# The first batch's work as one flat list of steps, in a quantized gated feed-forward kernel

## The chip, the cores and the metric

The kernel runs on one core of one Trainium2 chip. The metric is the device time in microseconds of one execution; a kernel's time is the median of its runs. The engines are named PE (matrix engine), PEld (its weight loads), ACT (scalar engine), DVE (vector engine), POOL (GpSimd) and SP (sync engine, which here only issues transfers). Each engine takes its instructions strictly in the order in which the program issues them to that engine, and waits at an instruction until what it needs is ready.

## The reference

Four batches of 1024 tokens, 512 wide, go through one gated feed-forward layer of 2048 hidden features whose hidden activations and down weights are quantized:

```python
scale = cond @ norm_w.T + 1.0
ms = jnp.mean(x * x, axis=-1, keepdims=True)
h = x * (scale[:, None, :] * jax.lax.rsqrt(ms + EPS))
u = h @ up_w.T
val, gate = jnp.split(u, 2, axis=-1)
h = val * jax.nn.gelu(gate, approximate=False)
hq = act_quant(h)       # per token: round(h * 127 / max|h|), clipped, scaled back
wq = weight_quant(down_w)   # round(w / mean|w|) to -1, 0, 1, times mean|w|
y = hq @ wq.T
return y + x
```

`x` is (4, 1024, 512), `cond` (4, 128), `norm_w` (512, 128), `up_w` (4096, 512), `down_w` (512, 2048), all float32.

## The kernel before

The hidden features are cut into 16 tiles `j` of 128 (`NJ`), the tokens of a batch into two halves `h` of 512. A slot is the work of one tile for one batch; `g = 16 * b + j` counts slots. Every float32 operand of the up projection is split into a high and a low float16 part, so that one product is three float16 products. PE sets the pace: from slot 14 on (`FAST = NJ - 2`) a slot does seven products (a Strassen scheme over the two token halves and gate and value; `product`, line 652) instead of the eight of the plain form (`plain`, line 667), and each later batch works its down projection in between.

The first batch, `b = 0`, is where everything else is prepared, beside PE:

- **Weights of tile j.** `w_load` (SP) brings them, `w_range` takes the largest or the sum of absolute values per row (from tile 3 on by ACT, line 304) and derives a power-of-two factor (`w_factor`, DVE, lines 161, 313, 319), `w_gain` makes the gains (DVE, lines 334, 337), `w_scale` scales the rows (ACT, line 349), `w_rows` splits them into high and low (ACT line 374, DVE line 375) and has them transposed by a transfer (SP, line 376) into one of three buffers `s_tile(j)`.
- **Sums for the fast form.** `s_sums` forms four sums of the weight blocks (POOL; DVE for tiles 14 and 15; lines 402 to 405) in a single scratch `sf`, `s_high` and `s_low` split them (ACT line 422, POOL line 426), `s_spill` writes all seven blocks to `s_dram`. Later batches read them back with `s_load`, in four pieces per slot.
- **Token sums of batch 0** for its two fast slots: `t0_whole` (line 677), `t0_sum` (680), `t0_high` (683) and `t0_low` (686), placed by the table `T0_STEPS` in slots 4 to 14.
- **Tokens of batch 1**, in four groups `a` of 128 pairs: class `Tokens` (load, norm, scale, sums, high, low, turn; lines 567 to 627). `turn` is one transposing transfer.
- **Conditioning rows of batches 1 to 3**: `cond_load_rest` broadcasts three rows of `cond` to all partitions (ACT's queue, line 182), `cond_scale_rest` multiplies and reduces them against `norm_w` on DVE (lines 203, 204) in slot 1; `cond_largest`, `cond_over`, `cond_range`, `cond_spread`, `cond_undo` and `cond_rows` turn them into scales.
- **Down weights**: `d_load`, `d_sum` (ACT, line 492) and `d_total`, `d_mean` find the mean; `d_fetch`, `d_round`, `d_sign` quantize.
- **Running maxima of the hidden values**: `pair_max` (DVE, lines 806 and 808).

One plain half-slot is `plain_half(j, h)`: twelve matmuls for the gate into a PSUM bank, the gelu of it on ACT (line 711), twelve matmuls for the value into another bank, and one DVE instruction that multiplies the two (line 715). The gate's bank is of tag B (one buffer) for half 0 and of tag A (two buffers) for half 1; the value's is of tag E (two buffers). So the gate of half 0 of a slot waits for the gelu of half 0 of the slot before, and a value waits for the DVE product of the half two before.

The order of the work around PE is written by hand: slots 1 and 2 line by line, slots 3 to 13 by the function `first_batch(j, sc)`, slots 14 and 15 by `first_fast(j)`. Where a helper has several instructions, they go out together: `w_range` issues ACT's sums and at once the DVE steps that need them, and `s_all` issues `s_high`, `s_low` and `s_spill` of a tile in a row. Ahead of slot 1 stands the head: loads, conditioning of batch 0, norms and transposes of the first 512 tokens, and filler matmuls (`keep_warm`, line 1079). Slots 16 to 63 and the end of the kernel have a planner of their own, which the change does not touch.

## Time and profile before

| | |
|---|---|
| median of 3 runs | 736.34 us (735.82 to 738.83) |
| the profiled execution | 737.17 us, span 735.4 us |
| granted PE clock, mean | 0.997 |
| PE busy | 718.5 us (98%), 3666 matmuls |
| DVE, ACT, POOL busy | 590.7, 419.4, 204.8 us |
| HBM read, written | 53.69 MB, 23.09 MB |

The span goes from the first to the last instruction of the profiled execution; the execution's own time is 1.8 us longer. A busy share is an average over stages with different limits, so the stretch that the change touches (about 21 us to 190 us of the span) is to be read by itself. In the rows of the profile, `L667` is a line of the kernel, `H<-pv,sg,g` are the tiles written and read, `x27` is a count, and `<-DVE H L715` names what ended a wait. SPq and ACTq are the issuing of transfers on SP's and ACT's queues.

### The profile page before, as it was taken

The numbers are of one execution on the slowest core, as the hardware profiler recorded it, in microseconds if no ns is written. First come the engines' busy times: TensorE is split into PE (matmuls) and PEld (weight loads), VectorE is DVE, ScalarE is ACT, GpSimd is POOL, SyncE is SP. The second block draws the span as 40 slices with busy tenths as digits, with TensorE's granted clock in tenths as the row PEclk, the third lists the DMA queues.
The fourth block names the chain that finished last, engine by engine and source line by source line (L and its number), as shares of the span: only waits on it lengthen the run. The fifth ranks groups of instructions, "written<-read, shape, count | busy, mean of one in ns | idle before, by whom it ended". The sixth has DMA issues, their size and how long they took to land.

```text
span 735.4 us, 10237 instructions
## 1 busy us (share of the span) xinstructions
PE 718.5 (98%) x3666; PEld 359.4 (49%) x3666; DVE 590.7 (80%) x828; ACT 419.4 (57%) x687; POOL 204.8 (28%) x201
## 2 busy tenths in 40 slices
PE   8999989989899999999999999999999999999998
PEld 3544434434344445665444444666444444444854
DVE  7855988979689889797679898687679888765896
ACT  6779657665666776544434667453333666333463
POOL 1477898783010030460010030452020000000120
PEclk9999999999999999999999999999999999999999
DMA  9689796989997546856955456666955464443243
GB/s 319 205 239 266 249 214 191 261 225 214 238 239 144 129 100 173 200 139 181 209 117 104 110 129 163 156 164 156 218 111 101 101 103 104 103 104 111 97 161 131
DMA packets 228542, 122.82 MB, mean 167 GB/s; under 512 B 189814, under 2 KB 199943, under 8 KB 228492
## 3 DMA queue, kind: packets, MB, share of 16 engines
q1 hardware_dynamic: 228202, 121.85, 66.5%
q8 instruction: 28, 0.46, 0.3%
q10 hardware_dynamic: 290, 0.33, 0.1%
q14 instruction: 22, 0.18, 0.1%
HBM read 53.69 MB, written 23.09 MB: 104 GB/s over the span
## 4 chain that ended last, share of the span: by engine, by line
PE 80%; POOL 6%; DVE 6%; DMA 2%; SPq 2%; issue 2%; ACT 1%; POOLq 0%; DVEq 0%; ACTq 0%
PE A L652 33%; PE E L652 17%; PE po L962 9%; PE B L652 8%; PE po_end L914 4%; PE pg L667 4%; PE pv L667 4%; DVE gm L806 1%; DMA H<-in_x_dram 1%; POOL R L426 1%; SPq L627 1%; POOL H L405 1%; POOL H L404 1%; DMA s_dram<-s_rows 1%; POOL xt L597 1%
## 5 line engine op out<-in xcount | busy, mean ns | idle before, releaser
L652 PEld LDWEIGHTS <-SXY 128*128 128x128 f16 x2058 | 201.4, 98 | 239.9 <-issue 3.3
L652 PE MATMUL A<-R,SXY 128*128 128x512 f16 x1158 | 268.2, 380 | 2.0 <-DMA SXY<-s_dram 2.0
L652 PE MATMUL E<-R,SXY 128*128 128x512 f16 x582 | 142.2, 380 | 0.3 <-DMA SXY<-s_dram 0.2
L770 DVE SCALAR_TENSOR_TENSOR H<-A,sg,t 128x512 f32<-128x512 f32 x50 | 37.5, 750 | 70.8 <-PE A L652 70.6
L822 POOL PARTITION_ALL_REDUCE am<-R x8 | 14.3, 1793 | 237.1 <-DVE R L808 237.1
L886 DVE TENSOR_TENSOR H<-H,am 128x1024 f32<-128x1024 f32 x64 | 76.1, 1215 | 0.0
L783 ACT ACTIVATE t<-t,sg 128x512 f32<-128x512 f32 x50 | 36.1, 721 | 67.6 <-DVE t L780 67.5
L652 PE MATMUL B<-R,SXY 128*128 128x512 f16 x294 | 71.5, 379 | 0.0
L667 PEld LDWEIGHTS <-SXY 128*128 128x128 f16 x438 | 42.7, 98 | 58.0 <-issue 7.0
L806 DVE TENSOR_REDUCE gm<-H 128x512 f32<-128x1024 f32 x56 | 69.0, 1233 | 1.1
L767 ACT ACTIVATE t<-B,sg 128x512 f32<-128x512 f32 x50 | 34.4, 687 | 37.8 <-PE B L652 37.8
L667 PE MATMUL pg<-R,SXY 128*128 128x512 f16 x228 | 52.4, 379 | 2.3 <-ACT g L711 2.3
L962 PE MATMUL po<-wd,R 128*128 128x256 fp8e4 x416 | 52.4, 273 | 0.0
L667 PE MATMUL pv<-R,SXY 128*128 128x512 f16 x210 | 48.9, 379 | 3.0 <-DVE H L715 3.0
L545 POOL TENSOR_SCALAR ssq<-ssq 128x2 f32<-128x2 f32 x12 | 3.4, 285 | 169.6 <-ACT xt L575 120.8
L750 ACT COPY t<-A 128x512 f32<-128x512 f32 x50 | 29.0, 580 | 34.4 <-PE A L652 34.1
L762 ACT COPY v<-E 128x512 f32<-128x512 f32 x50 | 29.3, 585 | 33.5 <-PE E L652 29.8
L962 PEld LDWEIGHTS <-R 128*128 128x128 bf16 (+1 forms) x448 | 43.8, 98 | 8.9
L757 ACT COPY B<-A 128x512 f32<-128x512 f32 x50 | 28.6, 572 | 29.1 <-PE A L652 28.6
L789 DVE SCALAR_TENSOR_TENSOR H<-v,sg,t 128x512 f32<-128x512 f32 x50 | 39.5, 791 | 6.3 <-ACT t L783 6.3
L808 DVE TENSOR_TENSOR R<-R,gm 128x512 f32<-128x512 f32 x56 | 42.6, 760 | 1.3
L894 ACT ACTIVATE H<-H 128x1024 f32<-128x1024 f32 x38 | 39.9, 1050 | 5.2 <-DVE H L886 5.2
(234 smaller groups left out, 1022.8 us busy)
## 6 DMA issues: line engine op xcount, KB each, us to landing
SXY<-s_dram SPq DMA_DIRECT2D x48, 256.0 KB, 3.1
H<-in_L_cond_up_w_dram SPq DMA_DIRECT2D x13, 512.0 KB, 4.6
s_dram<-SXY SPq DMA_DIRECT2D x17, 384.0 KB, 3.2
SXY<-s_dram SPq DMA_DIRECT2D x48, 128.0 KB, 3.2
xr<-in_x_dram SPq DMA_DIRECT2D x19, 256.0 KB, 3.0
out_dram<-xr SPq DMA_DIRECT2D x19, 256.0 KB, 2.4
H<-in_x_dram SPq DMA_DIRECT2D x8, 512.0 KB, 7.2
R<-in_L_cond_down_w_dram SPq DMA_DIRECT2D x8, 512.0 KB, 8.0
```

The lines of the kernel that those rows point to most:

```text
L652: PE.matmul(o, s[:, w, k, :], operand(g // NJ, c, l, k), start=start and n == 0, stop=stop and n == len(TERMS) - 1, skip_group_check=True,)
L667: PE.matmul(ps, a[k // 2][:, w, k % 2, :], XP[:, l, k, h * TOK : (h + 1) * TOK], start=n == 0, stop=n == len(terms) - 1,)
L767: ACT.activation(cur["t1"], pb, AF.Gelu, scale=gain(g, 1))
L770: DVE.scalar_tensor_tensor(h_half(g - 1, 0), prev["A"], gain(g - 1, 0), prev["t1"], ALU.mult, ALU.mult)
L783: ACT.activation(prev["t2"], prev["t2"], AF.Gelu, scale=gain(g - 1, 1))
L789: DVE.scalar_tensor_tensor(h_half(g - 1, 1), prev["v"], gain(g - 1, 0), prev["t2"], ALU.mult, ALU.mult)
L806: DVE.tensor_reduce(gm[0], v, AX.X, ALU.max, apply_absolute_value=True)
L808: return [largest, lambda: DVE.tensor_tensor(m, m, gm[0], ALU.max)]
L886: DVE.tensor_tensor(v, v, r.to_broadcast([P, 2, TOK]), ALU.mult)
L894: ACT.activation(v, v, AF.Copy, bias=MAGIC)
L914: PE.matmul(po.rearrange("p (y c o) -> p y c o", c=2, o=P), q[:, a, h, j], wd8[:, :, j // n, j % n, :, y0:y1].rearrange("p c o y -> p y c o"),
L962: PE.matmul(po, w[:, j], m, start=start and j == 0, stop=stop and j == n - 1, skip_group_check=True,)
```

## The change

The hand-written order from behind the first slot to the end of slot 15 is replaced by one flat list, `FIRST_BATCH`, that `take` walks through: each word is a step, with its arguments (`gate.4.1` is the gate of tile 4, half 1; `s_sum.5.1.1` is sum 1 of tile 5 on DVE, without the last 1 on POOL; `o_whole`, `o_sum`, `o_high`, `o_low` are the token sums of batch 0; `max` is `pair_max`; `c_...` are the conditioning steps; `slot.14.6` is step 6 of slot 14). The helpers are cut into single instructions for it: `s_sums` becomes four `s_sum`, `s_high`, `s_low` and `s_spill` take a part, `w_range` is apart from `w_factor`, `plain_half` becomes `half_gate`, `half_gelu`, `half_value` and `half_out`, `slot` uses a class `Slot` with the same products in the same order. PE's order of products is the one of before.

By the list, 37 of the 64 `s_sum`, 19 of the 32 `s_low` and 11 of the 16 `t_sum` are on DVE (before: 8 sums, and no `s_low` of the list's tiles). The token sums of batch 0 stand in slots 1 to 4 and use other scratch. `w_gain` from tile 3 on is on ACT. The first tokens of batch 1 and several weight tiles are loaded earlier; a number of spills stand later.

In the head, all four rows of `cond` are loaded at once, `norm_w` and `cond` are transposed on PE (`cond_turn`), and `cond_scale_rest` is four matmuls and one ACT instruction there; the broadcast load and the two DVE instructions of slot 1 are gone. From tile 3 on, `w_factor` writes the masked exponent beside a constant and takes the larger of the two by a reduction.

```diff
     ux = cpool.tile([P, B], F32, name="ux")
     nw = R[:, 1, 0:512].rearrange("p (k c) -> p k c", k=NK)
-    cb = R[:, 1, 512:1024].rearrange("p (b c) -> p b c", b=B)
+    nwT = R[:, 1, 512:1024]
     dots = R[:, 1, 1024 : 1024 + C]
...
-
+
+    def cond_turn():
+
+        pt = bank("E", 2, name="pc_t")
+        PE.transpose(pt[:, :B], cn, ident[:B, :B])
+        ACT.copy(cT, pt[:, :B])
+        pt = bank("E", 2, name="nw_t")
+        for k in range(NK):
+            PE.transpose(pt[:, k * P : (k + 1) * P], nw[:, k], ident)
+        ACT.copy(nwT, pt)
+
+    def cond_scale_rest():
+
+        n = B - 1
+        ps = bank("E", 2, name="ps")[:, : NK * n]
+        for k in range(NK):
+            PE.matmul(
+                ps[:, k * n : (k + 1) * n], nwT[:, k * P : (k + 1) * P], cT[:, 1:B],
+                start=True, stop=True,
+            )
+        v = ps.rearrange("p (k b) -> p k b", b=n)
+        ACT.activation(scT[:, :, 1:], v, AF.Copy, bias=1.0)
...
-    def cond_scale_rest():
-
-        n = B - 1
-        v = H[:, 9:11].rearrange("p s h t -> p (s h t)")[:, : n * NK * C]
-        v = v.rearrange("p (b k c) -> p b k c", b=n, k=NK)
-        s = cb[:, 1:].rearrange("p b (o c) -> p b o c", o=1).to_broadcast([P, n, NK, C])
-        w = nw.rearrange("p (o k) c -> p o k c", o=1).to_broadcast([P, n, NK, C])
-        DVE.tensor_tensor(v, w, s, ALU.mult)
-        DVE.tensor_reduce(scT[:, :, 1:].rearrange("p k b -> p b k"), v, AX.X, ALU.add)
...
-    def s_sums(j, eng=POOL):
+    def s_sum(j, n, eng=POOL):
...
-    TMP = [R[:, 1, n : n + 2 * TOK].rearrange("p (k t) -> p k t", k=2) for n in (7168, 5376, 3584)]
-    TMP.append(H[:, 15])
+    TMP = [H[:, 5], H[:, 9], H[:, 4], H[:, 10]]
...
-            DVE.tensor_scalar(sg0[:, c], sw[:, c], dx[:, 0:1], None, ALU.mult)
+            ACT.activation(sg0[:, c], sw[:, c], AF.Copy, scale=dx[:, 0:1])
...
-    ACT.dma_start(out=cn, in_=cond[0:1])
+    ACT.dma_start(out=cn, in_=cond)
...
     pc = cond_first_row()
+    cond_turn()
     keep_warm(5)
...
     root = rsqrt_root(0, 2)
+    cond_scale_rest()
     keep_warm(4)
...
-    cond_load_rest()
...
+    FIRST_BATCH = """
+        d_load.6 d_load.5 d_load.3 w_load.3 d_load.4 t_load.0 d_load.7 s_sum.0.0 o_whole.2.2.0 gate.1.0
+        x_scale.6 w_range.3 x_scale.7 s_sum.0.1 gelu.1.0 turn.4 turn.5 w_load.4 w_factor.3 s_sum.0.2 turn.6
+        w_range.2 turn.7 o_whole.0.0.0 w_load.5 x_high.0 value.1.0 x_high.3 x_low.0 d_load.2 x_high.1
+        s_high.0.0 w_factor.2 s_sum.0.3 w_load.9 x_high.2 s_low.0.0 x_low.1 w_scale.2.1 x_low.2 w_scale.2.0
+        x_low.3 gate.0.1 o_whole.1.0.1 w_scale.3.1 out.1.0 rows_high.2 value.0.1 gelu.0.1 rows_low.2
+        rows_turn.2 d_sum.4 s_sum.1.0 w_scale.3.0 gate.1.1 s_sum.1.1.1 rows_high.3 s_sum.1.2 c_largest
+        o_WHOLE.3.2.1 w_range.4 d_load.0 rows_low.3 value.1.1 gelu.1.1 s_high.0.1 t_square.0.0 s_low.0.1.1
+        s_spill.0.0 s_sum.1.3.1 s_high.1.0 w_factor.4 w_load.10 w_range.5 out.0.1 rows_turn.3 gate.2.0
+        s_low.1.0.1 s_high.1.1 w_scale.4.1 w_factor.5 s_low.1.1 out.1.1 d_sum.5 value.2.0 s_sum.2.1
+        w_scale.5.0 s_sum.2.0.1 w_scale.5.1 o_sum.0 d_sum.6 s_sum.2.2 c_over w_scale.4.0 gate.2.1 d_load.1
+        c_range s_sum.2.3 s_spill.1.0 rows_high.4 s_spill.2.1 d_sum.7 w_gain.2 o_sum.1 gelu.2.0 value.2.1
+        rows_low.4 o_high.1 out.2.0 w_gain.4 rows_high.5 o_low.1 w_load.6 gate.3.0 gelu.2.1 o_sum.2
+        s_high.2.0 rows_turn.4 s_high.2.1 o_sum.3 o_high.2 value.3.0 o_high.3 rows_low.5 s_spill.3.1
+        gelu.3.0 rows_turn.5 o_low.2 d_sum.2 gate.3.1 out.2.1 t_square.0.1 max.0.0.0 d_sum.3 t_root.0
+        d_sum.0 s_low.2.0.1 s_spill.2.0 value.3.1 o_low.3 w_range.6 s_sum.3.0 w_load.7 d_sum.1 s_spill.4.1
+        w_factor.6 s_low.2.1 w_load.11 w_scale.6.0 c_spread s_sum.3.1.1 s_spill.2.2 c_rows gate.4.0 out.3.0
+        o_high.0 w_scale.6.1 o_low.0 gelu.3.1 rows_high.6 out.3.1 value.4.0 s_sum.3.2.1 w_range.7 max.1.0.0
+        s_sum.3.3 w_load.8 s_high.3.1 rows_low.6 rows_turn.6 gelu.4.0 gate.4.1 s_high.3.0 s_low.3.0
+        s_low.3.1.1 c_copy w_factor.7 w_scale.7.1 max.0.1.0 w_scale.7.0 t_load.1 value.4.1 out.4.0 s_sum.4.0
+        rows_high.7 rows_low.7 rows_turn.7 gelu.4.1 w_range.8 gate.5.0 s_sum.4.1.1 d_total s_sum.4.2.1
+        out.4.1 s_high.4.0 s_sum.4.3.1 w_factor.8 s_spill.5.1 s_low.4.0 c_undo w_scale.8.1 c_store value.5.0
+        s_sum.5.1.1 s_spill.3.2 w_scale.8.0 s_spill.6.1 w_gain.6 c_load gelu.5.0 s_sum.5.0.1 rows_high.8
+        max.1.0.1 d_spread out.5.0 gate.5.1 w_range.9 rows_low.8 s_spill.7.1 s_high.4.1 s_low.4.1 max.1.1.0
+        value.5.1 rows_turn.8 s_sum.5.2.1 s_high.5.0 s_sum.5.3.1 c_bring gelu.5.1 max.1.1.1 s_high.5.1
+        s_low.5.0.1 gate.6.0 w_factor.9 s_sum.6.1 d_mean w_scale.9.0 t_scale.0.1 w_scale.9.1 out.5.1
+        s_spill.5.0 t_high.0.1 s_spill.3.0 t_scale.0.0 value.6.0 gelu.6.0 s_spill.8.1 max.2.0.0 t_sum.0.1
+        rows_high.9 s_low.5.1 t_high.0.0 s_sum.6.0.1 s_sum.6.2.1 s_high.6.0 gate.6.1 t_low.0.0 s_sum.6.3
+        t_sum.0.0.1 rows_low.9 value.6.1 rows_turn.9 gelu.6.1 max.2.0.1 w_gain.8 t_sum.0.2.1 w_range.10
+        t_sum.0.3 t_high.0.2 w_factor.10 gate.7.0 s_low.6.0.1 w_scale.10.1 out.6.0 w_scale.10.0 t_low.0.2
+        rows_high.10 s_spill.4.0 s_spill.5.2 value.7.0 t_low.0.1 t_turn.0 s_sum.7.1.1 out.6.1 rows_low.10
+        w_range.11 gate.7.1 s_sum.7.0.1 s_sum.7.2 s_high.6.1 s_low.6.1.1 t_square.1.0 max.2.1.0 t_square.1.1
+        s_sum.7.3 s_high.7.0 s_spill.4.2 t_root.1 value.7.1 s_spill.9.1 gelu.7.0 max.2.1.1 s_spill.6.0
+        s_high.7.1 s_low.7.1 rows_turn.10 w_factor.11 s_low.7.0.1 gate.8.0 s_sum.8.0.1 s_sum.8.2.1 out.7.0
+        gelu.8.0 max.3.0.0 s_spill.7.0 s_spill.6.2 value.8.0 s_sum.8.1.1 s_sum.8.3.1 w_gain.10 t_scale.1.1
+        gelu.7.1 s_high.8.0 s_low.8.0.1 s_spill.8.0 s_high.8.1 gate.8.1 w_scale.11.1 w_scale.11.0
+        s_sum.9.0.1 out.7.1 s_low.8.1.1 s_sum.9.2.1 value.8.1 s_sum.9.1.1 s_high.9.0 s_sum.9.3.1 w_load.12
+        t_sum.1.0.1 s_low.9.0.1 rows_high.11 s_spill.8.2 w_range.12 rows_low.11 rows_turn.11 gate.9.0
+        max.3.0.1 out.8.0 t_scale.1.0 value.9.0 s_spill.9.0 t_sum.1.1 gelu.8.1 t_load.2 gelu.9.0 w_factor.12
+        s_spill.11.1 out.8.1 w_scale.12.1 s_sum.10.0.1 w_scale.12.0 t_sum.1.2.1 gate.9.1 s_high.9.1
+        s_sum.10.1.1 rows_high.12 t_sum.1.3 max.3.1.0 s_spill.7.2 s_low.9.1 t_high.1.2 s_sum.10.2.1
+        max.3.1.1 t_high.1.1 value.9.1 s_high.10.0 s_sum.10.3.1 w_load.13 rows_low.12 t_high.1.0
+        rows_turn.12 t_low.1.1 s_high.10.1 t_low.1.2 gelu.9.1 gate.10.0 w_range.13 t_low.1.0 out.9.0
+        s_low.10.0.1 t_turn.1 value.10.0 max.4.0.0 s_sum.11.0 gelu.10.0 s_low.10.1 out.9.1 s_sum.11.2.1
+        s_sum.11.1.1 s_high.11.0 max.4.0.1 gate.10.1 s_sum.11.3.1 t_square.2.1 s_low.11.0.1 s_sum.12.0
+        s_spill.12.1 s_high.11.1 w_factor.13 w_load.14 s_spill.11.0 s_low.11.1.1 value.10.1 gelu.10.1
+        s_sum.12.2.1 s_spill.10.1 t_load.3 t_square.2.0 w_scale.13.0 t_root.2 w_scale.13.1 s_sum.12.1
+        gate.11.0 t_scale.2.1 out.10.0 t_high.2.1 s_spill.9.2 rows_high.13 t_scale.2.0 rows_low.13
+        rows_turn.13 s_high.12.0 value.11.0 w_range.14 s_low.12.0.1 s_sum.13.1 t_high.2.0 out.10.1 gate.11.1
+        w_factor.14 s_sum.12.3 w_scale.14.1 s_spill.10.2 t_low.2.1 s_sum.13.0.1 s_spill.10.0 w_scale.14.0
+        t_sum.2.1.1 s_spill.11.2 t_sum.2.0.1 w_gain.12 value.11.1 s_spill.12.0 s_sum.13.2.1 gelu.11.0
+        t_sum.2.2 t_sum.2.3.1 w_load.15 gelu.11.1 s_high.12.1 out.11.0 s_high.13.0 s_low.13.0 s_spill.13.0
+        out.11.1 gate.12.0 t_low.2.0 t_high.2.2 value.12.0 gelu.12.0 t_low.2.2 w_range.15 t_turn.2
+        s_low.12.1 max.4.1.0 t_square.3.0 s_sum.14.1 gate.12.1 t_square.3.1 s_sum.13.3.1 w_factor.15
+        rows_high.14 t_root.3 s_sum.14.0.1 max.4.1.1 s_sum.14.2 rows_low.14 value.12.1 gelu.12.1
+        rows_turn.14 w_scale.15.1 w_scale.15.0 out.12.0 out.12.1 rows_high.15 gate.13.0 s_high.13.1
+        s_high.14.0 d_fetch.0 s_low.13.1.1 w_gain.14 t_scale.3.1 gelu.13.0 s_sum.14.3.1 s_low.14.0.1
+        s_turn.14.0 value.13.0 t_scale.3.0 s_high.14.1 s_sum.15.0 rows_low.15 t_high.3.0 s_spill.14.0
+        t_high.3.1 rows_turn.15 d_round.0 t_sum.3.0.1 gate.13.1 t_sum.3.1.1 s_low.14.1.1 s_sum.15.1
+        w_gain.15 t_sum.3.2.1 s_spill.13.1 t_sum.3.3.1 s_turn.14.1 s_sum.15.2 max.5.0.0 t_high.3.2
+        value.13.1 s_sum.15.3 gelu.13.1 out.13.0 s_spill.15.1 s_high.15.0 s_low.15.0.1 s_spill.14.2
+        s_turn.15.0 slot.14.0 gains t_low.3.2 slot.14.2 out.13.1 d_fetch.1 slot.14.1 t_low.3.0 slot.14.4
+        t_low.3.1 t_turn.3 slot.14.3 slot.14.6 slot.14.5 s_high.15.1 s_low.15.1 slot.14.7 slot.14.13
+        slot.14.14 slot.15.0 slot.15.1 max.5.0.1 s_spill.15.0 s_load.16.0 slot.15.2 s_turn.15.1 slot.15.6
+        slot.15.7 s_load.16.1 slot.14.8 slot.14.9 s_load.17.0 s_spill.15.2 d_round.1 d_fetch.2 slot.15.4
+        s_spill.13.2 d_sign.0 d_fetch.3 max.5.1.0 slot.14.10 slot.15.5 max.5.1.1 slot.15.13 s_load.17.1
+        slot.14.11 slot.14.12 slot.15.3 slot.14.15 d_sign.1 max.6.0.0 s_load.16.2 d_fetch.5 slot.15.14
+        d_fetch.4 max.6.0.1 s_spill.14.1 s_load.16.3 max.6.1.0 s_spill.12.2 max.6.1.1
+    """
...
-    for j in range(3, FAST):
-        if j == 4:
-            sc = cond_load_scale(1)
-        if j == 5:
-            cond_bring(1, sc)
-        first_batch(j, sc if j >= 4 else None)
-    for j in range(FAST, NJ):
-        first_fast(j)
...
+    take(FIRST_BATCH)
```

More of the change, by code (lines that the diff above doesn't have):

```diff
@@ L607, in parts, with place @@
             ]
-        def high(self):
+        def place(self):
             if self.nx_at is None:
@@ L1384, in glu_quant_kernel @@
[L1384 to L1407 removed]
+    toks, ams, made = {}, {}, {}
```

608 lines of the change are left out of this document (263 added, 345 removed).

## Prediction

> **What bounds the kernel now.** I read the page first, then who waits for whom on PE.
>
> ```profile
> PE 718.5 (98%) x3666; PEld 359.4 (49%) x3666; DVE 590.7 (80%) x828; ACT 419.4 (57%) x687; POOL 204.8 (28%) x201
> PE pv L667 <- DVE H L715: 4.3, 5, 1.4
> PE pg L667 <- ACT g L711: 3.5, 3, 1.2
> PE A L652 <- DMA SXY<-s_dram: 2.0, 1, 2.0
> ```
>
> PE is busy for 98% of the span, and the change takes no product away. So it can only win back time in which PE stands idle or runs slowly. Of its waits, 7.8 us fall on the plain halves of the first batch (value banks held by line 715, gate banks by the gelu) and 2.0 us on the hand-over to slot 16. The timeline of PE with the chain of waits (which gives start-to-start lengths) says what a perfect order would save.
>
> ```profile
> 21.11 2.89 PE L667 MATMUL pg<-R,SXY 128*128 128x512 f16 x12
> 24.00 1.75 PE ptx L1063 x16
> 28.34 2.59 PE pg L667 x12
> 59.46 0.38 PE L242 MATMUL pd<-dg,one 3*128 3x3 f32 x2
> 173.16 1.46 PE L652 MATMUL A<-R 128*128 128x512 f16 x6
> 187.56 1.46 PE L652 MATMUL A<-wd,SXY 128*128 128x512 f16 x6
> 191.03 2.23 PE L652 MATMUL A<-R,SXY 128*128 128x512 f16 x6 [2.01 <-DMA SXY<-s_dram]
> 195.49 1.46 PE L652 MATMUL B<-R,SXY 128*128 128x512 f16 x6
> ```
>
> From 21.11 (slot 1) to 173.16 (slot 14) pass 152.05 us. PE's work there is 27 halves of two blocks of 2.59, 139.86, plus 1.75 for the transposes and four small conditioning and mean steps of at most 0.38 (the row shown is the longest), 1.52: 143.13. The loss is 8.9 us, the waits and the restarts behind them. At the hand-over, from 187.56 to 195.49, three products of 1.295 (half of 2.59) take 7.93 instead of 3.88: 4.05 us lost, twice the wait, because the six matmuls behind it take 2.23 instead of 1.46. Both together, 13.0 us, are all that the list can win.
>
> The busy time by stretches says who is late.
>
> ```profile
> core 0: us, PE busy (x) PEld busy (x) DVE busy (x) ACT busy (x) POOL busy (x), PEclk, DMA share, GB/s
> 21.11:70.27 49.16, 49.16 (x237) 23.13 (x236) 28.03 (x57) 40.40 (x77) 32.16 (x34) 1.00 0.77 230
> 70.27:173.16 102.89, 95.06 (x436) 42.46 (x436) 93.31 (x110) 68.49 (x129) 86.11 (x78) 1.00 0.86 224
> 104.51:207.00 102.49, 95.07 (x426) 41.73 (x426) 87.00 (x104) 65.72 (x114) 61.95 (x58) 0.98 0.94 230
> 182.00:197.00 15.00, 12.79 (x52) 5.05 (x51) 10.89 (x13) 6.75 (x9) 0.38 (x1) 0.89 1.05 256
> ```
>
> In slots 1 to 4 (21.11 to 70.27) PE never waits, and DVE is idle for 21 us. From slot 5 on all of the loss occurs, and DVE has 93.31 us to do beside 95.06 of PE, with 9.6 us of its own waiting. DVE, in its fixed order, is the late engine. The granted clock of 0.89 at the hand-over is the slow restart.
>
> Part of DVE's load is waiting for POOL.
>
> ```profile
> 93.54 2.69 DVE L686 TENSOR_TENSOR wd<-R,wd 128x1024 f16<-128x1024 f32 x1
> 181.43 1.23 DVE L686 TENSOR_TENSOR wd<-H,wd 128x1024 f16<-128x1024 f32 x1 [0.68 <-ACT wd L683]
> 160.97 0.94 DVE L403 TENSOR_TENSOR H<-H 128x256 f32<-128x256 f32 x1
> 171.85 0.41 DVE L404 TENSOR_TENSOR H<-H 128x256 f32<-128x256 f32 x1
> 170.31 0.94 DVE L375 TENSOR_TENSOR H<-H 128x768 f16<-128x768 f32 x1
> L680 DVE TENSOR_TENSOR R<-R 128x1024 f32<-128x1024 f32 x3 | 7.0, 2319 | 0.0
> L686 DVE TENSOR_TENSOR wd<-R,wd 128x1024 f16<-128x1024 f32 x3 | 5.2, 1735 | 0.0
> L161 DVE TENSOR_TENSOR wam<-wam,emask 128x2 int32<-128x2 int32 x14 | 5.8, 416 | 16.7 <-ACT H L304 16.7
> L337 DVE TENSOR_SCALAR sg<-sw,dx 128x4 f32<-128x4 f32 x7 | 4.3, 618 | 0.0
> L313 DVE SCALAR_TENSOR_TENSOR sw<-wam,undo 128x2 f32<-128x2 f32 x14 | 6.5, 468 | 0.5
> 163.22 0.15 DVE L161 TENSOR_TENSOR wam<-wam,emask 128x2 int32<-128x2 int32 x1
> L624 DVE TENSOR_TENSOR nx<-xt,nx 128x1024 f16<-128x1024 f32 x4 | 6.5, 1613 | 0.0
> L624 DVE TENSOR_TENSOR nx<-xa,nx 128x256 f16<-128x256 f32 x2 | 3.3, 1648 | 0.0
> L624 DVE TENSOR_TENSOR nx<-xn,nx 128x512 f16<-128x512 f32 x2 | 2.3, 1154 | 0.0
> 92.82 0.72 POOL L599 TENSOR_TENSOR xt<-xn,xt 128x256 f32<-128x256 f32 x1
> 93.51 1.64 POOL L426 TENSOR_TENSOR SXY<-H,SXY 128x768 f16<-128x768 f32 x1
> ```
>
> The same shape takes 2.69 us while POOL works and 1.23 while it rests; a sum takes 0.94 and 0.41. The group of line 161 also shows what the order costs: 16.7 us of DVE idleness in front of `w_factor`, because `w_range` issues ACT's sums and the DVE step behind them together.
>
> **The change, part by part.** *DVE from slot 5 on.* Out go the token sums of batch 0 (7.0 and 5.2, and two `t0_whole` of the same size at no less than 1.23 each, say 2.9: together 15.1), six `w_gain` of 0.618 (3.7) and the eight sums of slots 14 and 15 (half at about 0.94, half at 0.41, less a little overlap: 4.9). 93.3 − 23.7 = 69.6. In come 43 sums (32 of weights, 11 of tokens), eight `s_low` of 768 elements, four of 256 and three of 512. Instructions that follow each other overlap by about 0.07 us, so a sum costs 0.34 undisturbed and 0.87 disturbed. Undisturbed: 43 × 0.34 = 14.6, and 8 × 0.87 + 4 × 0.34 + 3 × 0.55 = 10.0 for the `s_low` (0.55 lies between the two sizes shown). That makes 94.2. Against it stands relief: POOL keeps some 20 sums of 0.72, 8 `s_low` of 0.7 to 1.64 and three roots in this stretch, so its 86.1 us fall to about 25, from 84% of the time to 27%. What DVE paid for POOL is, by the rows shown, 8.0 us in lines 161 and 313 (14 times 0.416 + 0.468 less two of 0.15 to 0.16), and 1.5, 2.5 and 1.1 in line 624 (against 1.23, 0.41 and 0.62): 13.1. Two thirds of it, 8.8, go: 85.4. If 27% of the moved instructions are disturbed, 43 × 0.27 × 0.53 = 6.2 and 10.0 × 0.27 × 1.2 = 3.2 for the `s_low` (the ratio 2.69 to 1.23 is 2.2) come on top: 94.8. I take 87.6, a quarter of the way up: the disturbed row, at 160.97, belongs to three such sums in a row, the worst case shown.
>
> The Trainium skill, SBUF — State Buffer, section Who interferes with whom, states that a VectorE instruction with two SBUF inputs and a GpSimd instruction that reads SBUF exclude each other, and that the one issued second blocks until the first ends. The trace agrees: line 686, started at 93.54, ran 2.69, and POOL's instruction from 93.51 took 1.64 (1.64 + 1.23 = 2.87). The rule speaks against moving 58 such instructions to DVE; where every one met a POOL instruction it would give the rival "port" below.
>
> DVE's own waiting, 9.6 us before, I leave as it is, though the list sets `w_range` well ahead of `w_factor`; it stands for waits of DVE on ACT that are new. 87.6 + 9.6 = 97.2 against 102.9: **−5.7 us** of the 8.9. Ends: −8.9 (PE never waits) and a loss (rivals).
>
> *Slots 1 to 4.* DVE gets the token sums of batch 0 there (four sums and four low parts at about 1.2, one `t0_whole`), five sums and four `s_low`: some 15 us into 21 us of idleness: nothing. ACT gets four casts of the token sums (1.04 each, line 683 below), two more `w_range`, two more tiles' `w_scale` and two more row casts, all 1024 elements wide and taken as the same 1.04: 10.4 us onto 40.4, so 50.8 in 49.2. It falls some 2 us behind, and a gate of half 0 waits only if the gelu of half 0 of the slot before is late by most of the three blocks between them (7.8 us). Nothing, with that cover; up to 2 us without it. `w_load.3` now stands behind three down-weight loads, one of which needs the scratch of the last norm:
>
> ```profile
> L683 ACT CAST wd<-R 128x1024 f16<-128x1024 f32 x3 | 3.1, 1040 | 2.1 <-DVE R L680 2.1
> 17.47 0.63 ACT L1029 ACTIVATE R<-H 128x512 f32<-128x512 f32 x1
> 9.66 0.38 SPq L288 DMA_DIRECT2D H<-in_L_cond_up_w_dram  x1
> 7.88 1.68 PE L1079 MATMUL pz<-H 128*128 128x512 f16 x7
> 10.75 2.14 PE L1063 MATMUL ptx<-ident,H 128*128 128x128 f32 x16 [1.18 <-ACT H L1056]
> 181.06 6.79 SPq L627 DMA_TRANSPOSE R<-nx  x1
> 188.52 1.50 SPq L458 DMA_TRANSPOSE SXY<-s_dram  x1
> ```
>
> so it goes out at about 18.5 instead of 9.66, and lands near 23, just when `w_range.3` wants it: nothing to 0.5 us.
>
> *The head.* PE gets five transposes (0.13 each by the 16 in 2.14) and four small float32 matmuls (0.38 each, after line 242): 2.2 us ahead of fillers that end at 9.56. The first transpose, which waits until 10.75, could start at 11.8; but the last of the 16 waits for a later norm anyway. 0 to 1.0, I take **+0.3**. The two DVE instructions and the load that go lay under idle time: nothing.
>
> *The hand-over.* Before, the last token turn held SP from 181.06 for 6.79 us, and the loads of slot 16 stood behind it; the transposing one left at 188.52, and slot 16 was due at 188.85. In the list that turn stands right behind DVE's last low part, beside slot 14, and two of the four loads stand close behind it; but DMA is at 0.94 of its time from 104.51 on and at 1.05 at the hand-over, and the batch before gets shorter. Between 0 and all of 4.05; I take half: **−2.0 us**.
>
> Sum: −5.7 + 0.3 − 2.0 = −7.4 us. The profiled execution took 737.17 us, 0.83 more than the median of 736.34; taken off the one it gives 729.8, off the other **728.9 us**.
>
> **The rivals.** *PE-bound.* All loss goes: 736.34 − 13.0 = 723.3. For it: PE did not wait in slots 1 to 4 though ACT worked 40.4 of 49.2 us. Against: DVE at 87.6 of 93 us of PE work. *Hand-over unchanged.* SP is held as before and five spills and fetches stand between the loads of slots 16 and 17: 736.34 − 5.7 + 0.3 = 730.9. *The waits only move.* DVE's load is the upper 94.8, and its 9.6 us of waiting stay: 104.4, 1.5 more than now; with +0.3 and −2.0, 736.1. The list would then not do what it says, and the waits would have new names. *Port (slower).* In slots 5 to 13 each moved instruction meets POOL half of the time and nothing is relieved: the added work is the mean of 24.6 and 59.4 (sums at 0.87, `s_low` 2.2 times as long), 42.0; 69.6 + 42.0 + 9.6 = 121.2, and DVE is the bound: 18.3 us more in the stretch, less 1.7 elsewhere, 752.9. It decides from the point where DVE's work passes the 93.3 of before. Against it: POOL is left with about a quarter of its time.
>
> **How the numbers follow.** Forecast 0.50, PE-bound 0.08, hand-over unchanged 0.14, waits only move 0.14, port 0.14. A measurement of this kernel can tell about 0.5%, 3.7 us, from no change: faster is under 732.7, slower over 740.0. Faster: 0.50 + 0.08 + 0.14 = 0.72; same 0.14; slower 0.14. The range goes from 723.0, just under the PE bound, to 738.0, which takes in the moved waits with the upper cost of the head (0.7 more) and a little of their spread, and leaves out the port case and a little of each end.
>
> **What would show it.** Right: PE's waits for lines 715 and 711 under 4 us together; L161 idle far below 16.7; POOL's busy total down by some 60 us; slot 14's first product near 167, slot 16's near 184. Wrong: DVE rows of `s_sum` at 0.9 rather than 0.4, PE waiting on line 715 more than 4.3 us; gates of slots 3 to 5 waiting for the gelu (ACT late); the wait for `s_dram` at the hand-over as long as before.

## The result, and the profile after

The kernel after takes **726.71 us** (median of 4 runs, 724.39 to 728.48) against 736.54 for the kernel before (4 runs, 735.82 to 738.83): a ratio of the means of **0.9859 [0.9823, 0.9896]**, 1.4% faster. 728.9 was predicted, within 723.0 to 738.0. The profiled execution took 727.31 us, with a span of 725.4 us (before: 735.4).

The page of the kernel after, its busy totals and its chain of what ended last:

```profile
PE 718.4 (99%) x3679; PEld 362.7 (50%) x3679; DVE 584.5 (81%) x876; ACT 419.9 (58%) x697; POOL 139.1 (19%) x143
...
PE 93%; DVE 4%; ACT 1%; DMA 1%; issue 0%; SPq 0%
```

PE is busy for as long as before, POOL does 65.7 us less, and PE alone carries 93% of the chain. PE's waits (line, what it waited for, us in total, times, longest) show that none of the three waits of before is left:

```profile
PE pz L1172 <- DVE eps L1102: 1.5, 1, 1.5
PE pg L708 <- ACT R L1160: 1.3, 2, 0.9
PE pg L779 <- ACT SXY L411: 0.7, 1, 0.7
PE pg L779 <- ACT R L1160: 0.2, 1, 0.2
```

The first and the last two belong to the head, as before. New is only the second, in which PE waits for tokens that ACT prepares (line 1160). PE's timeline shows where it falls, and the marks by which the span can be cut (first product of slot 1, of slot 14, third product of slot 16):

```profile
23.25 2.86 PE L708 MATMUL pg<-R,SXY 128*128 128x512 f16 x12
...
31.04 0.38 PE L708 MATMUL pg<-R,SXY 128*128 128x512 f16 x1 [0.37 <-ACT R L1160]
32.35 2.32 PE L708 MATMUL pg<-R,SXY 128*128 128x512 f16 x10 [0.94 <-ACT R L1160]
...
167.35 1.46 PE L693 MATMUL A<-R 128*128 128x512 f16 x6
...
182.89 1.46 PE L693 MATMUL A<-R,SXY 128*128 128x512 f16 x6
...
185.48 1.46 PE L693 MATMUL B<-R,SXY 128*128 128x512 f16 x6
```

The marks account for the whole difference. Before, they stood at 21.11, 173.16 and 195.49; behind the last one both profiles have 539.9 us to go.

| us | before | after | difference |
|---|---|---|---|
| head, up to slot 1 | 21.11 | 23.25 | +2.14 |
| slots 1 to 13 | 152.05 | 144.10 | −7.95 |
| slot 14 to slot 16's third product | 22.33 | 18.13 | −4.20 |
| the rest | 539.9 | 539.9 | 0 |
| span | 735.4 | 725.4 | −10.0 |

So more was won than predicted in two places, and a part of it was lost in the head. The busy times by stretches, cut where slots 1 to 4 and slots 5 to 13 lie in this kernel (as in the prediction: the window, its length, busy time and instructions of PE, PEld, DVE, ACT and POOL, the granted clock, the DMA share, GB/s):

```profile
23.25:73.98 50.73, 49.42 (x238) 23.19 (x237) 42.31 (x71) 46.62 (x87) 22.83 (x21) 1.00 0.96 279
73.98:167.35 93.37, 93.37 (x435) 42.52 (x434) 81.07 (x150) 64.58 (x128) 30.17 (x34) 1.00 0.91 233
```

From slot 5 on PE is busy without a gap. DVE has 81.07 us to do there (before 93.31) and POOL 30.17 (before 86.11); DVE's idle 21 us in slots 1 to 4 have shrunk to 8.4. The groups of DVE's instructions from 21.11 to 175 us (count, then busy time and mean ns, then idle time ahead of them):

```profile
L432 DVE TENSOR_TENSOR H<-H 128x256 f32<-128x256 f32 x37 | 15.9, 441 | 2.2 <-POOL SXY L453 1.8
L453 DVE TENSOR_TENSOR SXY<-H,SXY 128x768 f16<-128x768 f32 x6 | 6.0, 1000 | 0.2 <-ACT SXY L449 0.2
L328 DVE TENSOR_TENSOR undo<-wam,undo 128x2 int32<-128x2 int32 x13 | 3.1, 235 | 5.3 <-ACT H L318 5.3
L720 DVE TENSOR_TENSOR H<-H 128x1024 f32<-128x1024 f32 x4 | 4.9, 1214 | 0.0
L726 DVE TENSOR_TENSOR wd<-H,wd 128x1024 f16<-128x1024 f32 x4 | 4.9, 1224 | 1.0 <-ACT wd L723 1.0
```

37 weight sums on DVE take 0.441 us each, close to the 0.41 of an undisturbed one and far from 0.94. The token sums take 1.214 (before 2.319), their low parts 1.224 (1.735), and DVE idles 5.3 us ahead of `w_factor` (line 328) where it idled 16.7 us. In slots 5 to 13 alone, this idle time fell from 6.9 to 1.9 us.

### The profile page after: what moved, and what is told of

Same layout as the page of the kernel before. It is cut to its first block, busy times and chain, and to the rows that moved or that the text cites. A ratio compares the mean times of both kernels' runs of the same rounds, so it can differ in the third digit from the quotient of the medians.

```text
span 725.4 us, 10231 instructions
## 1 busy us (share of the span) xinstructions
PE 718.4 (99%) x3679; PEld 362.7 (50%) x3679; DVE 584.5 (81%) x876; ACT 419.9 (58%) x697; POOL 139.1 (19%) x143
## 4 chain that ended last, share of the span: by engine, by line
PE 93%; DVE 4%; ACT 1%; DMA 1%; issue 0%; SPq 0%
PE A L693 33%; PE E L693 17%; PE pv L708 9%; PE po L1055 9%; PE pg L708 9%; PE B L693 9%; PE po_end L1007 4%; DVE gm L899 1%; PE pz L1172 1%; DMA H<-in_L_cond_up_w_dram 1%; DVE R L901 1%; DVE R L894 1%; ACT R L1160 1%; DVE H L828 0%; DVE t L836 0%
## 5 line engine op out<-in xcount | busy, mean ns | idle before, releaser
L845 DVE TENSOR_TENSOR v<-A,v 128x512 f32<-128x512 f32 x50 | 34.1, 683 | 13.1 <-PE A L693 11.9
L901 DVE TENSOR_TENSOR R<-R,gm 128x512 f32<-128x512 f32 x56 | 40.7, 727 | 1.0
```

Source lines behind the costliest of these rows:

```text
L845: DVE.tensor_tensor(self.v, self.A, self.v, ALU.add)
L901: return [largest, lambda: DVE.tensor_tensor(m, m, gm[0], ALU.max)]
```

## The experiments

The same three marks can be read in every profile, and the stretch behind the last of them is 539.9 to 540.0 us in all but one. That gives the yardstick for the experiments: 142.5 us for slots 1 to 13 and 18.13 us for the hand-over (slot 14 to slot 16's third product) are what PE takes when it never waits.

| profiled execution | slot 1 at | slots 1 to 13 | hand-over | span |
|---|---|---|---|---|
| before | 21.11 | 152.05 | 22.33 | 735.4 |
| after | 23.25 | 144.10 | 18.13 | 725.4 |
| weight range and factor joined | 23.86 | 156.29 | 18.13 | 738.2 |
| sums back on POOL | 21.00 | 152.32 | 18.52 | 731.8 |
| token sums late | 24.54 | 149.72 | 22.04 | 736.2 |
| last token turn late | 23.19 | 144.05 | 18.23 | 726.0 |
| old conditioning | 20.62 | 147.26 | 18.13 | 725.9 |
| before, with the new head | 24.40 | 151.35 | 20.44 | 736.1 |
| load of tile 3 first | 20.52 | 142.53 | 18.13 | 721.1 |
| high part 2 first | 23.04 | 143.74 | 18.13 | 724.9 |
| both first | 23.15 | 142.48 | 18.13 | 723.7 |
| fewer fillers | 21.76 | 144.38 | 18.13 | 724.2 |
| both first, fewer fillers | 21.83 | 142.48 | 18.13 | 722.4 |
| both first, turns later | 20.02 | 142.48 | 18.13 | 720.6 |

(The exception is the late turn, 540.5.) Every median below is of 4 or more executions, and every ratio is of the means, against executions of the kernel before taken beside it, whose medians lay from 735.4 to 736.5 us. Each kernel has one profile, so a row of the table is one execution.

**Weight range and factor joined.** For tiles 3 to 15 the DVE steps of `w_factor` stand right behind ACT's sums of `w_range`, as the kernel before issued them; all else is the list's.

```diff
-    ... w_range.11 gate.7.1 s_sum.7.0.1 ... rows_turn.10 w_factor.11 ...
+    ... w_range.11 w_factor.11 gate.7.1 s_sum.7.0.1 ... rows_turn.10 ...
```

> The changed kernel with every DVE factor step set directly behind the ACT sums of its tile, from tile 3 on, as before the change; all else of the list unchanged. Theory 'separation': DVE's waiting in front of the factor step comes back (5.3 us in the changed kernel, 16.7 before), its products come late, and PE waits 3 us or more for them; 730 us or more. Rival 'spread': what counts is that the token sums of batch 0 left the late slots; DVE now has 14% of the stretch free, the waits of DVE grow but PE's stay under 1 us, and the time stays within 1 us of the changed kernel.

Measured: 738.04 us (736.89 to 740.54), 1.0037 [1.0022, 1.0051]. The whole gain is gone. The same group of DVE's instructions:

```profile
L328 DVE TENSOR_TENSOR undo<-wam,undo 128x2 int32<-128x2 int32 x13 | 3.2, 246 | 19.2 <-ACT H L318 19.2
```

and one of the longest stalls in the timelines of DVE and PE:

```profile
124.99 0.16 DVE L328 TENSOR_TENSOR undo<-wam,undo 128x2 int32<-128x2 int32 x1 [3.73 <-ACT H L318]
...
127.19 0.74 DVE L764 SCALAR_TENSOR_TENSOR H<-pv,sg,g 128x512 f32<-128x512 f32 x1
127.99 2.75 PE L708 MATMUL pv<-R,SXY 128*128 128x512 f16 x12 [3.54 <-DVE H L764]
```

DVE does the same work, but stands 19.2 us ahead of line 328 instead of 5.3. In the stall shown it waits 3.73 us for ACT's sum with the product of gate and value (line 764) queued behind it, and PE waits 3.54 for that. In slots 5 to 13, DVE stands 12.3 us ahead of this line, against 1.9. Against the kernel after, 12.2 us are lost in slots 1 to 13. One wait of 2.6 us among them is a special case: tile 3's weights land late (below), and DVE, held by its factor, was late with a scaling that the token transposes needed.

**Sums back on POOL.** The order is the list's, but `s_sum`, `s_low` and `t_sum` go to the engine that had them before.

```diff
-    ... s_sum.7.1.1 out.6.1 rows_low.10 ... s_low.6.1.1 ... t_sum.1.0.1 ...
+    ... s_sum.7.1 out.6.1 rows_low.10 ... s_low.6.1 ... t_sum.1.0 ...
```

> The changed kernel with the weight sums, their low parts and the token sums on POOL as before the change (the sums of tiles 14 and 15 on DVE); same list otherwise. Theory 'port': POOL's work goes back to about 118 us in slots 1 to 13, the POOL chain of a tile (sums, low parts) takes over 10 us a slot and holds back the scratch, DVE's two-input instructions lengthen again (line 161's kind 0.42 us instead of 0.24), and PE waits come back: 732 us or more. Rival 'spread': DVE has 25 us less to do, and the time stays within 2 us of the changed kernel.

Measured: 735.75 us (733.32 to 737.44), 0.9995 [0.998, 1.0011]. The later slots of the first batch by busy time:

```profile
70.27:165.00 94.73, 89.58 (x404) 40.05 (x403) 63.69 (x90) 60.52 (x121) 74.08 (x80) 0.96 0.78 204
```

and the longest stall in the timelines, followed back from PE to DVE, ACT and POOL:

```profile
121.30 5.28 PE L708 MATMUL pv<-R,SXY 128*128 128x512 f16 x12 [5.15 <-DVE H L764]
117.79 2.20 DVE L398 TENSOR_TENSOR H<-H 128x1024 f16<-128x1024 f32 x1 [9.73 <-ACT H L394]
116.72 1.04 ACT L394 CAST H<-H 128x1024 f16<-128x1024 f32 x1
115.98 0.83 ACT L449 CAST SXY<-H 128x768 f16<-128x768 f32 x1 [3.01 <-POOL H L432]
114.54 2.09 POOL L432 TENSOR_TENSOR H<-H 128x256 f32<-128x256 f32 x3
```

DVE has only 63.69 us to do in 94.73 (before, 93.31 in 102.89), and yet slots 1 to 13 take as long as before. POOL's sums (the three shown took 2.09 us together) end late, ACT's cast of them waits 3.01 us, the cast of the weight rows queued behind that cast is late, DVE waits 9.73 us for it, and PE 5.15; the twelve matmuls behind the stall take 5.28 instead of 2.75. This one stall and the slow matmuls behind it make 7.7 of the 9.8 us by which slots 1 to 13 exceed the yardstick. DVE's load was therefore not what bound PE in this order; POOL's lateness reached PE through two in-order queues. The moved instructions lengthen DVE's work and shorten the chain.

**Token sums late.** The token sums of batch 0 go back to slots 4 to 14, to their old scratch and engines; all else is the list's.

```diff
-    ... value.3.1 o_low.3 w_range.6 ...
+    ... value.3.1 w_range.6 ... value.4.0 o_WHOLE.0.0.0 o_WHOLE.1.0.1 ... value.4.1 o_sum.0 ... slot.14.5 o_low.0 ...
```

> The changed kernel with the token sums of batch 0 back in slots 4 to 14, in their old scratch and on their old engines. Theory 'spread': 15 us of DVE work go back into slots 4 to 13, DVE's load there rises from 82 to about 97 us of 95 us of PE work, and PE waits come back: 730 to 736 us. Rival 'separation': the order of the other steps is what counts; the time rises by under 1.5 us.

Measured: 736.97 us (734.1 to 739.23), 1.0008 [0.999, 1.0025]. PE's waits for the product of gate and value are back, from 105 us on and into slot 14:

```profile
PE pv L708 <- DVE H L765: 3.3, 5, 1.3
PE E L693 <- DVE H L765: 2.1, 1, 2.1
PE pg L708 <- ACT g L755: 1.1, 1, 1.1
```

and so is DVE's load of the later slots:

```profile
70.27:165.00 94.73, 90.24 (x416) 40.44 (x415) 87.75 (x149) 65.90 (x127) 30.39 (x33) 1.00 0.81 214
```

DVE's work in the later slots is 87.75 us of 94.73, though PE did fewer matmuls there (416 against 442 in the same window of the kernel after, where DVE has 82.04). POOL has as little to do as in the kernel after (30.39 us), so in these slots it is DVE's load by itself. The wait in slot 14 is of another kind: DVE stood 3.33 us, until 170.18, for a token sum that is on POOL again and that POOL began only at 168.03, behind a transfer; the product of gate and value came behind it and other work in DVE's queue. Each of the three parts, undone alone, gives back 5.6 to 12.2 us in slots 1 to 13 out of 7.95: their worths don't add, and the gain needs all three. It says nothing of another order searched for without one of them.

**Last token turn late.** The turn that held SP at the hand-over, and the first load of slot 16, are put behind the last transposes of slot 15.

```diff
-    t_low.3.1 t_turn.3 slot.14.3 ... s_spill.15.0 s_load.16.0 slot.15.2 s_turn.15.1 slot.15.6
+    t_low.3.1 slot.14.3 ... s_spill.15.0 slot.15.2 s_turn.15.1 t_turn.3 s_load.16.0 slot.15.6
```

> The changed kernel with the last token turn (5.2 us on SP's queue) and the first load of slot 16 moved behind the last transpose of the sums of tile 15, about the order of before the change. Theory 'queue': the two loads that slot 16 needs leave some 3 us later, at 179 and 181 instead of 175.7 and 177.6, PE waits 1 to 3 us at the hand-over and runs slowly behind it: 2 to 4 us more than the changed kernel. Rival 'early': the hand-over got free because everything upstream is early; the turn's place costs under 0.5 us.

Measured: 727.6 us (726.83 to 728.1), 0.9888 [0.987, 0.9906]; with 726.71 (724.39 to 728.48) for the kernel after, no difference can be told. SP's queue in this kernel, and PE's one wait there:

```profile
175.01 4.31 SPq L668 DMA_TRANSPOSE R<-nx  x1
179.42 0.53 SPq L481 DMA_DIRECT2D SXY<-s_dram  x1
180.00 1.49 SPq L479 DMA_TRANSPOSE SXY<-s_dram  x1
...
193.79 1.47 PE L693 MATMUL E<-R,SXY 128*128 128x512 f16 x6 [0.39 <-DMA SXY<-s_dram]
```

The turn goes out 7.8 us after slot 14's first product, just as before (181.06 against 173.16: 7.9); in the kernel after it went out at 169.78, 2.4 us after. But it holds SP for 4.31 us instead of 6.79, the loads go out at once behind it, and only 0.39 us (0.6 with the restart) are lost. So the hand-over is not saved by the turn's earlier place alone. What else saved it is not settled: the list moved many spills, and no run separated them.

**Old conditioning.** The list stays; the conditioning rows go back to the broadcast load and two DVE instructions in slot 1.

```diff
-    ACT.dma_start(out=cn, in_=cond)
+    ACT.dma_start(out=cn[:1], in_=cond[0:1])
-    cond_turn()
...
-    cond_scale_rest()
...
+    cond_load_rest()
...
-        ... s_sum.1.2 c_largest ...
+        ... s_sum.1.2 c_scale c_largest ...
```

> The flat list as changed, with the conditioning rows of batches 1 to 3 as before the change: broadcast load on ACT's queue, two DVE instructions (1.97 and 1.75 us) in slot 1, no transposes and no small matmuls in the head. Theory 'head': the additions to PE's queue in the head put slot 1 off by 2.1 us, so slot 1 starts near 21.1 us instead of 23.25 and the kernel is 2.1 us faster than the changed one, about 724.6 us; the DVE work in slot 1 costs nothing. Rival 'relief': taking 3.7 us off DVE in slot 1 is what keeps the early slots free of waits; then PE waits appear in slots 1 to 3 and the gain is under 1 us or a loss.

Measured: 727.15 us (726.35 to 727.66), 0.9879 [0.9863, 0.9895], the same as the kernel after. Slot 1 begins 2.63 us earlier, at 20.62, but 4.8 us are lost in slots 1 to 13 instead of 1.6:

```profile
PE pv L711 <- DVE H L767: 1.1, 2, 0.9
PE pg L711 <- DVE R L1167: 1.0, 1, 1.0
PE pg L711 <- DMA SXY<-H: 0.7, 1, 0.7
...
24.68 1.95 DVE L331 TENSOR_TENSOR undo<-wam,undo 128x2 int32<-128x2 int32 x1 [1.42 <-ACT H L321]
...
35.23 1.74 DVE L205 TENSOR_TENSOR cprod<-R 128x1536 f32<-128x1536 f32 x1
```

Only a part of this is shown to come from the two instructions. They run on DVE from 35.23 to 38.76. The longest wait of the first row, 0.90 at 43.48, stands behind them: DVE works there almost without a gap up to the product that PE needs. The wait of the second row, at 30.52, comes before them. There DVE's factor step of tile 3 (line 331) took 1.95 us, against 0.55 in the kernel after, and ended at 26.63, just as a sum that POOL had begun at 24.50 ended, at 26.62. So in this profile slot 1 begins earlier and the early slots lose it again, and how much of that the conditioning costs on DVE is open.

**Before, with the new head.** The other way round: the kernel before, with the conditioning rows in its head and its own order of steps.

```diff
-    ACT.dma_start(out=cn, in_=cond[0:1])
+    ACT.dma_start(out=cn, in_=cond)
...
+    cond_turn()
...
+    cond_scale_rest()
...
-    cond_load_rest()
...
-    cond_scale_rest()
```

> The kernel before with only the conditioning rows moved into the head (transposes and eight small products on TensorE, the sum on ScalarE), its order of steps as it was. Theory (the move costs the head its time and gives nothing back in the old order, since VectorE had 21 us of idleness in slots 1 to 4): slot 1 begins 0.5 to 2.5 us later than the 21.11 of before, the waits on the value halves stay near 4 us and the time is 736.5 to 739. Rival (the move relieves VectorE and ScalarE also in the old order): 733 to 735, with the waits on the value halves under 3 us.

Measured: 737.59 us (734.43 to 739.31, 10 runs), 1.0009 [0.9993, 1.0026]. By itself the new head brings nothing to the old order. Its hand-over took 20.44 us in the profile, though the order of steps is that of the kernel before (22.33); so some of the loss there differs without the list. Its ten times fall into two groups, four from 734.4 to 735.8 and six from 737.5 to 739.3, and the profiled one, of the second group, shows what may part them. PE's fillers and transposes in the head:

```profile
3.72 1.09 PE L188 MATMUL nw_t<-ident,R 128*128 128x128 f32 x4
...
6.95 1.71 PE L196 MATMUL ps<-R 128*128 128x3 f32 x8
8.51 1.87 PE L1089 MATMUL pz<-H 128*128 128x512 f16 x4
...
10.83 3.17 PE L1089 MATMUL pz<-H 128*128 128x512 f16 x7
```

The last seven fillers took 1.68 us in the kernel before, 0.24 each; here they take 3.17, 0.45 each. PE works at half its rate until about 15 us.

**Load of tile 3 first** and **high part 2 first.** Two single steps of the list, each moved alone, against the one wait that is left in slots 1 to 13.

```diff
-        d_load.6 d_load.5 d_load.3 w_load.3 d_load.4 ...
+        w_load.3 d_load.6 d_load.5 d_load.3 d_load.4 ...
```
```diff
-        x_high.1 s_high.0.0 w_factor.2 s_sum.0.3 w_load.9 x_high.2 ...
+        x_high.1 x_high.2 s_high.0.0 w_factor.2 s_sum.0.3 w_load.9 ...
```

> The changed kernel with the load of weight tile 3 at the head of the list, as before the change, ahead of the three down-weight loads. Theory 'transfer': ACT waits 2.64 us for that tile ahead of the casts of the second token half, and that is why the gate of tile 0, half 1 waits 1.3 us; with the earlier load the wait goes and the kernel takes about 1.5 us less, 725.2 us. Rival 'order': the cast of the sums that stands ahead of the last token cast on ACT makes the wait; then about 0.7 us of the 1.3 stay.

> The changed kernel with the last cast of the second token half moved ahead of the cast of the weight sums on ACT (0.84 us). Theory 'transfer': the cast still comes too late by the 2.6 us for which ACT waited earlier; the wait of the gate falls only from 1.3 to about 0.5 us, the kernel takes 0.8 us less. Rival 'order': the whole wait goes, 1.5 us.

Measured: 724.65 us (722.91 to 726.09), 0.9852 [0.9827, 0.9877], and 724.37 us (724.18 to 726.65), 0.9849 [0.9829, 0.9869]. SP's queue and ACT's order in the kernel after explain both:

```profile
8.26 12.45 SPq L511 DMA_DIRECT2D R<-in_L_cond_down_w_dram  x3
20.76 0.43 SPq L302 DMA_DIRECT2D H<-in_L_cond_up_w_dram  x1
...
27.34 0.63 ACT L318 ACTIVATE H<-H 128x512 f16<-128x512 f32 x1 [2.64 <-DMA H<-in_L_cond_up_w_dram]
...
30.87 0.84 ACT L449 CAST SXY<-H 128x768 f16<-128x768 f32 x1
31.59 0.71 ACT L1160 ACTIVATE R<-ptx,scT 128x512 f16<-128x512 f32 x1
```

The load of tile 3 stands behind three down-weight loads that hold SP from 8.26 to 20.7; it leaves at 20.76, ACT waits 2.64 us for it, and the high parts of the second half's tokens (line 1160), which PE needs, are late behind that, one of them also behind a cast that is not due yet. With the load first (it leaves at 7.80) both waits are gone and slots 1 to 13 take 142.53, as theory 'transfer' expected; with the high part first the wait falls from 1.3 to 0.6 us, but slots 1 to 13 only from 144.10 to 143.74. The times say less than the traces, since slot 1 began at 20.52 in the one profile and at 23.04 in the other.

**Both first, fewer fillers, turns later.** Four more kernels ask what the head costs. One cuts the fillers of the kernel after (`keep_warm(4)` and `(7)` to 2 and 2). One makes both moves above. One makes both and cuts the fillers. The last makes both moves, puts the transposes of the conditioning behind twelve fillers and its small products behind all of them, and drops two of the last seven:

```diff
     pc = cond_first_row()
-    cond_turn()
     keep_warm(5)
...
-    cond_scale_rest()
     keep_warm(4)
+    cond_turn()
...
-    keep_warm(7)
+    keep_warm(5)
+    ps = cond_dots_rest()
...
+    cond_scale_rest(ps)
     w_scale(0, (1,))
```

> The changed kernel with 7 of the 16 fillers behind the transposes of the head left out (4 and 7 become 2 and 2). Theory 'queue': the fillers stand in PE's order ahead of the first token transposes, so that 2.2 us of new PE work only delays them; without those fillers the token transposes start near 10.8 us instead of 13.16, slot 1 near 21.1, and the kernel takes about 724.6 us. Rival 'clock': the fillers are needed to bring PE to speed; then the first matmuls of slot 0 take 0.4 us each instead of 0.22, and the gain is under 1 us.

> The kernel after with two steps of the list moved: the load of weight tile 3 ahead of the down-weight loads, and the high part of token block 2 ahead of the first weight sum's high part. Theory (the two early waits have separate causes and their gains add, less what the one has already taken): no wait on a line of slots 1 to 13, 142.5 us from slot 1 to slot 14, 723 to 725 by when TensorE takes up its full rate in the head. Rival (one gain contains the other, since both relieve ScalarE at the same place): the same time as the earlier load alone, 724.7, within 0.5.

> The same two steps moved, and the filler products in the head cut from four and seven to two and two. Theory (fillers that TensorE works at half its rate are pure delay there, and the token transposes need no more of them): slot 1 near 21.0 to 21.8 in every execution, 722.5 to 724, with a spread under 1 us. Rival (fewer fillers delay the full rate into the first plain half): slot 1 at 23 or later, or plain matmuls of slot 0 at half rate, 725 or more.

> The same two steps moved, and in the head the five conditioning transposes stand behind twelve filler products instead of three, and the eight small products behind all fillers (five instead of seven in the last group). Theory (the transposes and three-column products in the midst of the fillers are what delays TensorE's full rate in some executions): the full rate is there by 8.3 us as in the kernel before, the seventh to twelfth filler takes 0.24 us in each execution, slot 1 begins at 20.5 to 21.2, and the time is 722.0 to 723.5 with a spread under 1 us. Rival (the moment is a matter of chance or of the count of products alone): slot 1 again between 20.5 and 24 from one execution to the next, 723 to 726.

Measured: fewer fillers 725.92 us (725.79 to 726.25), 0.9864 [0.9849, 0.9878]; both first 725.54 (723.61 to 725.8), 0.9846 [0.9832, 0.9861]; both and fewer fillers 725.33 (724.45 to 725.78), 0.9848 [0.9833, 0.9862]; both and turns later **723.11 (722.37 to 723.42), 0.9818 [0.9803, 0.9832]**, the best of all kernels run. With both first no wait is left in slots 1 to 13, as expected, yet three of its four times lie above the expected 725; in its profile slot 1 begins at 23.15. Fewer fillers narrow the spread (0.5 and 1.3 us), but the medians miss what was expected, 724.6 and 722.5 to 724: slot 1 begins at 21.76 and 21.83, and with both moves the median stays within 0.2 us of that of both first. The head of the last kernel:

```profile
3.66 1.96 PE L1175 MATMUL pz<-H 128*128 128x512 f16 x5
5.71 1.02 PE L1175 MATMUL pz<-H 128*128 128x512 f16 x4
...
6.81 0.66 PE L189 MATMUL nw_t<-ident,R 128*128 128x128 f32 x4
...
7.71 1.25 PE L1175 MATMUL pz<-H 128*128 128x512 f16 x5
8.79 0.95 PE L197 MATMUL ps<-R 128*128 128x3 f32 x8
...
20.02 2.87 PE L711 MATMUL pg<-R,SXY 128*128 128x512 f16 x12
```

Within the first five fillers PE comes to its full rate; the same transposes take 0.66 us instead of 1.08, the eight small products 0.95 instead of 1.71, and slot 1 begins at 20.02. Its four spans lie from 720.6 to 721.6 us, so slot 1 began within 1.0 us in all of them if the rest took as long as in the profile; the spread of the times, 1.05 us, is just over the expected 1.

## Why the prediction was right, and where its terms were off

**What bounds the kernel** was right: only PE's lost time could be won, 13.0 us by the prediction. Without any wait slots 1 to 13 take 142.5 (143.1 was worked out) and the hand-over 18.13 instead of 22.33, which makes 13.8 us. The kernel after won 12.15 of it.

**DVE from slot 5 on, −5.7 us: the sign and the mechanism were right, the size too small.** The slots won 7.95 us net of the 1.6 us lost behind tile 3's late weights, so 9.6 from there on: the whole loss. The busy time came to 81.07 instead of 87.6, and so under the 85.4 that had been worked out for moved instructions that nothing disturbs. The sums were indeed hardly disturbed (0.441 against 0.41), and the relief was larger than the two thirds taken: the two instructions of lines 161 and 313 took 9.4 us for the eight tiles of this stretch, and the two that follow them (lines 328 and 330) take 2.8, partly because they were rewritten. (Two slips of the sum change little: the 8.0 us for lines 161 and 313 counted all 14 tiles where the stretch has eight, at 6.9, and a quarter of the way from 85.4 to 94.8 is 87.75.) POOL's 30.17 us came near the 25 worked out. With the measured load the prediction's own sum, 81.07 + 9.6 = 90.7, already lies under the 93.37 us of PE, so this term alone takes it to the bound. The step "DVE's own waiting, 9.6 us before, I leave as it is" failed too: undone alone, the distance between range and factor cost more than either of the other two parts, with DVE's work unchanged. The prediction also ranked DVE's load as the cause. The run with the sums on POOL loses as much as the kernel before with DVE at 63.69 us; there the chain from POOL over ACT to DVE sets the wait. The port rule of the Trainium skill (SBUF — State Buffer, Who interferes with whom), which the prediction weighed, is borne out: the token sums fell from 2.319 to 1.214 us when POOL had less to do, in the run with their old slots and scratch as well (1.214 for three of the four), and where POOL was kept busy again, DVE's low part of the weight rows took 1.465 us on the mean instead of 1.243.

**Slots 1 to 4, "nothing".** For ACT's load this held (46.62 us in 50.73). For `w_load.3`, "nothing to 0.5 us", it failed: the three down-weight loads held SP until 20.7, not 18.5, the weights were 2.64 us late for ACT, and PE lost 1.6 us with what stood behind. The earlier load removes it.

**The head, +0.3 us (0 to 1.0): mis-sized, +2.14 in the profile.** The four small float32 products, eight matmuls in the trace, took 1.71 us where 4 × 0.38 = 1.52 had been taken, and the four large transposes 1.08 where 0.13 each had been taken: both ran at PE's half rate. The larger part is a step that the prediction did not have: the fillers behind them stayed at half rate too (2.53 us for seven instead of 1.68, 1.87 for four instead of 1.62). Where the full rate came early, as in the load-first run, slot 1 began at 20.52, and the head cost nothing.

**The hand-over, −2.0 us (0 to 4.05): the upper end came true**, −4.20. The reason given, the turn's earlier place, does not carry it: the run that put the turn back lost only 0.6 us of it. What brought the rest is open, so that the term's upper end came true is luck as far as is known.

**The signs named ahead.** Waits on the value and gate banks under 4 us: none is left. Idle time at the factor far below 16.7: 5.3. POOL down by 60 us: 65.7. Slot 14 near 167: 167.35. Slot 16 near 184: its first product stands at 182.89. The median lies 2.2 us under the forecast and 3.4 us over the PE-bound rival (723.3), which the kernel with both steps first and the turns later reaches (723.11). The port rival and the moved waits did not happen.

## What to carry to other kernels

When an engine's instructions are strictly in order, look at what stands behind each wait before looking at busy times: an order that issues a producer on one engine well ahead of its consumer on the other was worth more here than taking load off the busiest helper. A move to an engine that is less loaded pays only if the chain behind it gets shorter, so follow the longest stall back through every queue. And where an engine starts at half its rate, look in the trace at when the full rate comes before pricing work in the head by its own length alone.
